# A scan layer's last unit: its sum taken part by part of the positions, its last product on two engines

## The chip, the cores and the metric

The kernel runs on one core of a Trainium2 chip. The metric is the device time of one execution in microseconds. In the text PE is TensorE, PEld its weight loads, DVE is VectorE, ACT ScalarE, POOL GpSimd, and SP the engine that issues the transfers between HBM and the on-chip memory SBUF. PSUM is the memory that TensorE writes its results to.

## The reference

Eight images of 192 channels, 64 x 64 pixels, fp32, go through four blocks one after the other: a block with a selective scan, a block without one, a second selective scan with a norm, and a block of windowed convolutions. The scan is what the change touches. For each of four directions through the image, each channel and each of 16 states:

```python
def step(h, inp):
    u_t, d_t, B_t, C_t = inp
    h = jnp.exp(d_t[..., None] * A) * h + (d_t * u_t)[..., None] * B_t[:, :, None, :]
    y = jnp.einsum('bkdn,bkn->bkd', h, C_t)
    return (h, y)
```

So a decay and an input are formed for every position and state, a first-order recurrence runs along the 4096 positions, and at every position the 16 states are multiplied by the 16 values of C and summed. Two of the four directions are the other two read backwards; the results of all are added.

## The kernel before, in words

An image is worked on as a whole before the next one starts: scan layer, the stages of the first and second block, scan layer, and then the stages behind the second scan of this image mixed with those ahead of the first scan of the next. That makes 16 scan layers in an execution. Each stage is in its own set of buffers and ends in HBM; between a scan layer and the stage behind it stand the tensors `ys` in HBM.

A scan layer (`scan_layer`) is cut into 48 units: two directions `d` (forward, then backward), eight chunks of Q = 512 positions, and three groups `v` of 128 rows (192 channels in two orders of the image). The last unit, number 47, is the backward one of the first chunk, group 2. A unit's states stand in one tile `da` of 128 partitions x 4 parts x 16 states x 128 positions; three such tiles take turns. A part (`s` or `g`) is 128 consecutive positions; in the backward direction the parts are worked on in falling order, so that the last part of unit 47 has place 0.

The loop over `k` (unit) and `j` (0 to 7) writes down by hand in which order the instructions stand; every engine runs its own in this order, and each waits only for the data and buffers that it needs. In step `j` of unit `k`:

- `scan` (L308, on DVE) runs the recurrence over 8 of the 16 states of one part, so two steps make a part. Its input is filled into PSUM by TensorE one step ahead (`fill`, L287).
- `times_c` (L319, on POOL), in every second step, multiplies a finished part by C, which `load_c` has broadcast from HBM into one of three tiles `ct`, issued by SP. Behind it, L322 (POOL too) adds the last states to the ones before them, so that 12 matmuls and a half one do for the sum instead of 16: for the first two parts the last four states, for the other two parts the last three. The product of a unit's fourth part stands in step 0 of the unit behind it.
- `add_up` (L337 and L342, on TensorE) sums the states of the unit before by matmuls with the identity into a PSUM tile `py`, of which there is one. A matmul of L337 takes one state over all four parts, 512 columns; L342 takes the thirteenth state of the last two parts, 256 columns. The list SUM says how many matmuls stand in each step.
- `load_y` (L328, SP) and `finish` (L352 or L356, DVE, and L357, SP) bring in the forward direction's result from `yp` where the unit is a backward one, add the sum to it and store the result to `ys`. `finish` of unit k stands in step 2 of unit k + 2, and `load_y` of unit k just behind `finish` of unit k - 1, in step 2 of unit k + 1. The tile `yo` has two buffers.

The loop runs over `nu + 2` = 50 places, so that the last two units are brought to their end; in the last two places there is nothing else left to do. `misc` is a PSUM tile of 512 columns with two buffers, used for transpositions (L229, L186) and small projections. The stage behind reads `ys` from HBM at L600 or L785 (or first loads weights for the next image, at L482), and it is issued by SP behind the last store at L357.

Line numbers in what follows are those of the profile of the kernel before.

Of the kernel before, what the change touches and what calls it, by code (L numbers as in the profile page):

```python
# [9 lines left out]
ALU = mybir.AluOpType  # L10
# [11 lines left out]
NS = 16  # L22
SB = 128
NB = Q // SB
# [16 lines left out]
def tile_net(ctx: ExitStack, tc: tile.TileContext, a: dict, out: bass.AP):  # L41
    nc = tc.nc
# [5 lines left out]
    ident = cst.tile([P, P], F32, name="ident")  # L48
# [50 lines left out]
    def scan_layer():  # L99
# [5 lines left out]
        with (  # L105
# [13 lines left out]
            NP = 12  # L119
            units = [  # L120
                (d, i, i if d == 0 else nck - 1 - i, v)
                for d in range(2) for i in range(nck) for v in range(3)
            ]
            vt, xd, cdr, dg = {}, {}, {}, {}
            dts, dtx, dtt, das, cts, us, py, yo = {}, {}, {}, {}, {}, {}, {}, {}

# [4 lines left out]
            def misc():  # L131
                return sp.tile([P, Q], F32, tag="misc", name="misc", bufs=2)


            def load_v(m):
                d, c, cols = chunk_of(m)
                vt[m] = sv.tile([P, 3, Q], F32, tag="vt", name="vt", bufs=3)
                for v in (2, 0, 1):
                    nc.sync.dma_start(out=vt[m][:, v, :], in_=vs[v][:, cols])
# [52 lines left out]
            def diagonals_b(m, o, r):  # L192

                shape = [P, 4, NS // 2, 32]
                at = slice(r * 4, (r + 1) * 4)
                nc.vector.tensor_tensor(  # L196
                    dg[m, o][:, at], msk[:, 0:32].unsqueeze(1).unsqueeze(1).to_broadcast(shape),
                    bts[m, o][:, at, r * 8 : r * 8 + 8].unsqueeze(3).to_broadcast(shape), ALU.mult,
                )
# [19 lines left out]
            def steps_c(k):  # L219
                dtx[k] = sw.tile([P, Q], F32, tag="dtx", name="dtx")  # L220
                nc.gpsimd.tensor_tensor(dtx[k], dts[k], vt[k // 3][:, units[k][3], :], ALU.mult)  # L221
# [27 lines left out]
            def cut(k, s=slice(0, NB)):  # L249

                d = units[k][0]
                head = das[k][:, s, :, SB - 1 if d else 0]
                nc.scalar.copy(da0[:, k % 2, s], head)
                nc.scalar.mul(head, head, 0.0)  # L254
# [39 lines left out]
            def scan(k, j):  # L294
                d, i, c, v = units[k]
                s, n = place(k, j)
                last = 0 if d else SB - 1
                u = us.pop((k, j))
                if j > 1 or i:
                    if j % 2 == 0:  # L300
                        prev = das[k][:, s + 1 if d else s - 1, :, last] if j else carry[v]
                        tmps[k] = sw.tile([P, NS], F32, tag="tmp", name="tmp")
                        nc.vector.tensor_tensor(tmps[k], da0[:, k % 2, s], prev, ALU.mult)  # L303
                    head = u[:, :, SB - 1 if d else 0]
                    nc.vector.tensor_tensor(head, head, tmps[k][:, n], ALU.add)  # L305
                way = slice(None, None, -1 if d else 1)
                h = das[k][:, s, n].rearrange("p n t -> p (n t)")[:, way]
                nc.vector.tensor_tensor_scan(  # L308
                    h, h, u.rearrange("p n t -> p (n t)")[:, way], 0.0, ALU.mult, ALU.add
                )  # L310

            def keep(k):
                d, i, c, v = units[k]
                if i < nck - 1:
                    nc.scalar.copy(carry[v], das[k][:, 0 if d else NB - 1, :, 0 if d else SB - 1])

            def times_c(k, g):
                h = das[k][:, NB - 1 - g if units[k][0] else g]
                nc.gpsimd.tensor_tensor(h, h, cts.pop((k, g)), ALU.mult)  # L319
                n = NS - NP if g < 2 else NS - NP - 1  # L320
                to = h[:, NP - n : NP]
                nc.gpsimd.tensor_tensor(to, to, h[:, NS - n : NS], ALU.add)  # L322

            def load_y(k):
                d, i, c, v = units[k]
                yo[k] = sw.tile([P, Q], F32, tag="yo", name="yo")
                if d:
                    nc.sync.dma_start(out=yo[k], in_=yp[v][:, c * Q : (c + 1) * Q])  # L328
# [3 lines left out]
            def add_up(count):  # L332

                for k, n in to_add[:count]:
                    if n == 0:
                        py[k] = sp.tile([P, Q], F32, tag="py", name="py")
                    nc.tensor.matmul(  # L337
                        py[k], ident, das[k][:, :, n, :], start=(n == 0), stop=(n == NP - 1)
                    )
                    if n == 8:  # L340
                        s = slice(0, NB // 2) if units[k][0] else slice(NB // 2, NB)
                        nc.tensor.matmul(  # L342
                            py[k][:, s.start * SB : s.stop * SB], ident, das[k][:, s, NP, :],
                            start=False, stop=False,
                        )
                del to_add[:count]

            def finish(k):
                d, i, c, v = units[k]
                p, y = py.pop(k), yo.pop(k)  # L350
                if d == 0:
                    nc.vector.scalar_tensor_tensor(  # L352
                        y, vt[k // 3][:, v, :], skip[:, v : v + 1], p, ALU.mult, ALU.add
                    )
                else:
                    nc.vector.tensor_tensor(y, y, p, ALU.add)  # L356
                nc.sync.dma_start(out=(ys if d else yp)[v][:, c * Q : (c + 1) * Q], in_=y)  # L357

            nu, nm = len(units), len(units) // 3


            SUM = ((1, 0, 1, 2, 0, 2, 1, 2), (2, 2, 1, 1, 1, 2, 2, 2), (2, 1, 1, 2, 2, 2, 2, 2))
# [2 lines left out]
            def has(k):  # L365
                return 0 <= k < nu
# [24 lines left out]
                    fill(0, 0)  # L391
            for r in range(2):
                diagonals_b(0, 1, r)
            for k in range(nu + 2):
                m, v = divmod(k, 3)
                ahead = 0 <= m + 1 < nm
                for j in range(8):
                    if v == 1 and j == 3 and 0 <= m + 2 < nm:
                        load_v(m + 2)
                    if has(k):  # L400
                        scan(k, j)
                    if j == 7:
                        if has(k + 1):
                            cut(k + 1)
                        if has(k):
                            keep(k)
                    if j % 2 == 0:
                        kk, g = (k, j // 2 - 1) if j else (k - 1, 3)
                        if has(kk):
                            times_c(kk, g)  # L410
                        if has((4 * kk + g + 3) // 4):
                            load_c(*divmod(4 * kk + g + 3, 4))
                    if j == 5 and has(k + 2):
                        steps_c(k + 2)
                    kk, jj = (k, j + 1) if j < 7 else (k + 1, 0)
                    if has(kk):
                        fill(kk, jj)
                    if j == 2:
                        if has(k - 2):
                            finish(k - 2)  # L420
                        if has(k - 1):
                            load_y(k - 1)
                        if has(k + 1):
                            turn(k + 1)
                    if ahead and (v, j) == (0, 4):

                        steps_a(k + 3)
                        steps_a(k + 4)
                    if ahead and v == 1 and j == 1:

                        steps_b(k + 2)
                        steps_a(k + 4)
                        steps_b(k + 3)
                        steps_b(k + 4)
                    if v == 0 and ahead:
                        if j == 0:
                            project_a(m + 1)
                        if j == 1:
                            project_b(m + 1)
                    if v > 0 and ahead:  # L440
                        if j == (5, 1)[v - 1]:
                            diagonals_a(m + 1, v - 1)
                        if j >= 6:
                            diagonals_b(m + 1, v - 1, j - 6)
                    if j == 2 and has(k - 1):
                        to_add += [(k - 1, n) for n in range(NP)]
                    add_up(SUM[v][j])
                    if has(k + 1) and j in DECAY:
                        decay(k + 1, *DECAY[j])

# [852 lines left out]
```

## Time and profile before

| | us |
|---|---|
| median of three runs | 26363.84 |
| the three runs | 26368.85, 26363.84, 26362.46 |
| the profiled execution | 26345.77 |
| its span, first to last instruction | 26344.0 |

| engine | busy us | share of the span |
|---|---|---|
| PE | 23298.1 | 88% |
| PEld | 12085.3 | 46% |
| DVE | 20617.9 | 78% |
| ACT | 14204.8 | 54% |
| POOL | 19170.7 | 73% |

The mean granted clock of TensorE is 0.929 of full speed. How to read it: the shares are means over stages with different limits, the scan layers and what stands between them, so a change in one place is read from the rows of that place. A matmul in fp32 stands in the records as two, and a weight load goes with each; a record's duration is longer than the distance to the next, since records overlap. In a view in order of time several records of one line are drawn together, and the brackets hold the idle time ahead of the first one and what ended it. Groups are by line; `da`, `ct`, `py`, `yo` are the tiles named above.

### The profile page before, as it was taken

Reading aid. Unit: us, or ns where it says so; the run is one execution under the profiler, and the core shown is the slowest. Engines: PE = TensorE matmul, PEld = TensorE weight load, DVE = VectorE, ACT = ScalarE, POOL = GpSimd, SP = SyncE. Lnnn points to the kernel's source line nnn. Section 1 sums busy time; section 2 is a strip of 40 time slices with the busy share of each in tenths; the row PEclk is TensorE's granted clock in tenths of the full one; section 3 lists DMA queues with packets and bytes.
Section 4 is the critical chain, followed back from the end, with each engine's and each line's share of the span. In section 5 each row is a group of like instructions: output and inputs, shape, how many; then the busy total and the mean of one; then the engine's idle time right before and its main releaser. Section 6 shows DMA issues by size and latency. Waiting matters only on the chain.

```text
span 26344.0 us, 431326 instructions
## 1 busy us (share of the span) xinstructions
PE 23298.1 (88%) x173960; PEld 12085.3 (46%) x173960; DVE 20617.9 (78%) x21237; ACT 14204.8 (54%) x23120; POOL 19170.7 (73%) x7452
## 2 busy tenths in 40 slices
PE   9979889798897988979889898898989989899896
PEld 4535445353453534535345353453535535355353
DVE  7959789597885968859688696886968869688695
ACT  5646456464554645546455464554645546465463
POOL 7929589295892958939589395893958939588395
PEclk9989999899998999989999899998999989999898
DMA  5636556265563655636556365563656636566364
GB/s 168 206 92 201 148 174 205 92 203 149 171 201 96 203 145 175 200 96 202 143 177 205 93 203 139 181 201 93 203 137 182 200 96 204 134 186 197 99 204 119
DMA packets 1204798, 4293.86 MB, mean 163 GB/s; under 512 B 360224, under 2 KB 419456, under 8 KB 804480
## 3 DMA queue, kind: packets, MB, share of 16 engines
q1 hardware_dynamic: 1202816, 4266.25, 54.7%
q8 instruction: 1388, 22.74, 0.4%
q14 instruction: 594, 4.87, 0.1%
HBM read 3810.55 MB, written 450.72 MB: 162 GB/s over the span
## 4 chain that ended last, share of the span: by engine, by line
POOL 36%; PE 12%; DVE 7%; ACT 3%; issue 3%; DMA 2%; SPq 0%; POOLq 0%; DVEq 0%; ACTq 0%
POOL da L319 27%; POOL da L322 6%; PE py L337 3%; PE pa L501 2%; POOL dtx L221 2%; PE u L287 2%; DVE da L308 2%; PE pa L504 1%; ACT da L244 1%; DVE pwc L932 1%; DVE t L966 1%; DMA a<-t 1%; DMA t<-u 0%; PE paa L501 0%; PE pb L511 0%
## 5 line engine op out<-in xcount | busy, mean ns | idle before, releaser
L308 DVE TENSOR_TENSOR_SCAN da<-da,u 128x1024 f32<-128x1024 f32 x6144 | 14039.6, 2286 | 328.7 <-ACT da L254 37.9
L319 POOL TENSOR_TENSOR da<-da,ct 128x2048 f32<-128x2048 f32 x3072 | 13928.8, 4534 | 330.6 <-DVE tmp L303 302.2
L337 PE MATMUL py<-da,ident 128*128 128x512 f32 x18432 | 9494.1, 628 | 538.8 <-POOL da L319 437.4
L287 PEld LDWEIGHTS u<-dg,dtt 32*128 32x128 f32 x131072 | 5946.8, 163 | 4601.3 <-issue 4301.7
L244 ACT ACTIVATE da<-dt,neg_a 128x512 f32<-128x512 f32 (+1 forms) x12544 | 7662.2, 699 | 16.2
L287 PE MATMUL u<-dg,dtt 32*128 32x128 f32 x131072 | 7237.6, 283 | 118.0 <-DVE da L308 49.3
L337 PEld LDWEIGHTS py<-da,ident 128*128 128x128 f32 x18432 | 3122.1, 191 | 3138.8 <-issue 2239.7
L221 POOL TENSOR_TENSOR dtx<-dt,vt 128x512 f32<-128x512 f32 x768 | 979.5, 1276 | 4011.7 <-ACT dt L217 3747.0
L322 POOL TENSOR_TENSOR da<-da 128x512 f32<-128x512 f32 (+1 forms) x3072 | 3487.6, 1135 | 240.9
L231 ACT COPY dtt<-misc 128x512 f32<-128x512 f32 x768 | 450.4, 586 | 3338.3 <-PE misc L229 3338.3
L305 DVE TENSOR_TENSOR u<-u,tmp 128x8 f32<-128x8 f32 x5952 | 1007.6, 169 | 1092.7 <-PE u L287 869.8
L234 ACT COPY dtt<-misc 32x512 f32<-32x512 f32 x3008 | 1734.7, 577 | 45.2
L196 DVE TENSOR_TENSOR dg<-msk,misc 128x1024 f32<-128x1024 f32 x1024 | 1222.6, 1197 | 442.6 <-PE misc L186 258.7
L160 ACT ACTIVATE xd<-misc,msk 128x512 f32<-128x512 f32 x256 | 175.7, 686 | 1791.3 <-PE misc L156 1791.3
L217 ACT ACTIVATE dt<-misc 128x512 f32<-128x512 f32 x768 | 430.8, 595 | 1105.1 <-PE misc L213 1098.0
L914 PE MATMUL pwc<-t,l3taps 128*128 128x486 f32 (+1 forms) x1280 | 595.3, 614 | 234.4 <-DVE t L935 214.0
L920 POOL TENSOR_TENSOR acc<-u,gate 128x486 f32<-128x486 f32 (+1 forms) x80 | 108.4, 1360 | 949.5 <-DVE u L935 674.0
L876 POOL MEMSET t<- 128x4356 f32 (+2 forms) x32 | 100.6, 3145 | 934.3 <-DVE t L850 913.4
L501 PE MATMUL pa<-sqa,mean_w 128*128 128x512 f32 x384 | 306.5, 944 | 337.1 <-ACT sqa L541 337.1
L229 PE MATMUL misc<-ident,dtx 128*128 128x128 f32 x3072 | 594.2, 318 | 0.0
L186 PE MATMUL misc<-ident,xd 16*128 16x16 f32 x4096 | 565.6, 266 | 25.2 <-DVE dg L196 25.2
L186 PEld LDWEIGHTS misc<-ident,xd 16*128 16x128 f32 x4096 | 528.2, 210 | 92.6 <-issue 88.8
(286 smaller groups left out, 18307.8 us busy)
## 6 DMA issues: line engine op xcount, KB each, us to landing
ct<-cd SPq DMA_DIRECT2D x2048, 1024.0 KB
ct<-cd SPq DMA_DIRECT2D x2048, 512.0 KB
vt<-vs SPq DMA_DIRECT2D x768, 256.0 KB
yp<-yo SPq DMA_DIRECT2D x384, 256.0 KB
yo<-yp SPq DMA_DIRECT2D x384, 256.0 KB
ys<-yo SPq DMA_DIRECT2D x384, 256.0 KB
yt<-ys SPq DMA_DIRECT2D x96, 512.0 KB
t<-ys SPq DMA_DIRECT2D x96, 512.0 KB
```

What stands on the lines that cost most here:

```text
L186: nc.tensor.transpose(pt[:, i * NS : (i + 1) * NS], xd[m][rows, cols], ident[rows, rows])
L196: nc.vector.tensor_tensor(dg[m, o][:, at], msk[:, 0:32].unsqueeze(1).unsqueeze(1).to_broadcast(shape), bts[m, o][:, at, r * 8 : r * 8 + 8] ...
L221: nc.gpsimd.tensor_tensor(dtx[k], dts[k], vt[k // 3][:, units[k][3], :], ALU.mult)
L234: (nc.scalar.copy if k else nc.vector.tensor_copy)(dtt[k][q * 32 : (q + 1) * 32, 1], pt[r * 32 : (r + 1) * 32])
L244: nc.scalar.activation(das[k][:, s, n, :], dts[k].rearrange("p (s t) -> p s t", t=SB)[:, s], AF.Exp, scale=neg_a[:, v, d, n : n + 1],)
L287: nc.tensor.matmul(u[ch, r * 4 : r * 4 + 4, e::4], dtt[k][rows, r, e, ch], dg[k // 3, o][rows, r * 4 + e, n], start=True, stop=True,)
L305: nc.vector.tensor_tensor(head, head, tmps[k][:, n], ALU.add)
L308: nc.vector.tensor_tensor_scan(h, h, u.rearrange("p n t -> p (n t)")[:, way], 0.0, ALU.mult, ALU.add)
L319: nc.gpsimd.tensor_tensor(h, h, cts.pop((k, g)), ALU.mult)
L322: nc.gpsimd.tensor_tensor(to, to, h[:, NS - n : NS], ALU.add)
L337: nc.tensor.matmul(py[k], ident, das[k][:, :, n, :], start=(n == 0), stop=(n == NP - 1))
L501: nc.tensor.matmul(pa[:, h], w[0][:, c], src[0][:, h], start=True, stop=False)
```

## The change

For the last unit of each layer alone:

- Its sum is not made by `add_up` but by a new function `add_last`, part by part: the first two parts together (12 matmuls of 256 columns), then the third (13 of 128 columns), then the fourth (16 of 128 columns). It goes into a `misc` tile instead of the `py` tile.
- The product of its fourth part by C is cut in two: 8 states on POOL and 8 on DVE. The addition of L322 isn't made for this part.
- `load_y` of this unit stands in step 3 of the unit itself, and `finish` in step 2 of place 48. The loop has 49 places instead of 50.

The first two parts are summed behind the last full step of the unit, that is before the last matmul of unit 46; the third and fourth behind it.

```diff
--- before.py
+++ after.py
@@ -121,6 +121,7 @@
                 (d, i, i if d == 0 else nck - 1 - i, v)
                 for d in range(2) for i in range(nck) for v in range(3)
             ]
+            nu, nm = len(units), len(units) // 3
             vt, xd, cdr, dg = {}, {}, {}, {}
             dts, dtx, dtt, das, cts, us, py, yo = {}, {}, {}, {}, {}, {}, {}, {}
 
@@ -316,6 +317,12 @@
 
             def times_c(k, g):
                 h = das[k][:, NB - 1 - g if units[k][0] else g]
+                if k == nu - 1 and g == NB - 1:
+
+                    ct = cts.pop((k, g))
+                    for eng, n in ((nc.gpsimd, slice(0, 8)), (nc.vector, slice(8, NS))):
+                        eng.tensor_tensor(h[:, n], h[:, n], ct[:, n], ALU.mult)
+                    return
                 nc.gpsimd.tensor_tensor(h, h, cts.pop((k, g)), ALU.mult)
                 n = NS - NP if g < 2 else NS - NP - 1
                 to = h[:, NP - n : NP]
@@ -345,6 +352,19 @@
                         )
                 del to_add[:count]
 
+            def add_last(g0, g1):
+
+                k = nu - 1
+                if k not in py:
+                    py[k] = misc()
+                s = slice(NB - g1, NB - g0)
+                ns = NS if g1 == NB else NP + (g0 == 2)
+                for n in range(ns):
+                    nc.tensor.matmul(
+                        py[k][:, s.start * SB : s.stop * SB], ident, das[k][:, s, n, :],
+                        start=(n == 0), stop=(n == ns - 1),
+                    )
+
             def finish(k):
                 d, i, c, v = units[k]
                 p, y = py.pop(k), yo.pop(k)
@@ -356,7 +376,6 @@
                     nc.vector.tensor_tensor(y, y, p, ALU.add)
                 nc.sync.dma_start(out=(ys if d else yp)[v][:, c * Q : (c + 1) * Q], in_=y)
 
-            nu, nm = len(units), len(units) // 3
 
 
             SUM = ((1, 0, 1, 2, 0, 2, 1, 2), (2, 2, 1, 1, 1, 2, 2, 2), (2, 1, 1, 2, 2, 2, 2, 2))
@@ -391,7 +410,7 @@
                     fill(0, 0)
             for r in range(2):
                 diagonals_b(0, 1, r)
-            for k in range(nu + 2):
+            for k in range(nu + 1):
                 m, v = divmod(k, 3)
                 ahead = 0 <= m + 1 < nm
                 for j in range(8):
@@ -418,7 +437,9 @@
                     if j == 2:
                         if has(k - 2):
                             finish(k - 2)
-                        if has(k - 1):
+                        if k == nu:
+                            finish(k - 1)
+                        if has(k - 1) and k < nu:
                             load_y(k - 1)
                         if has(k + 1):
                             turn(k + 1)
@@ -442,9 +463,17 @@
                             diagonals_a(m + 1, v - 1)
                         if j >= 6:
                             diagonals_b(m + 1, v - 1, j - 6)
-                    if j == 2 and has(k - 1):
+                    if (k, j) == (nu - 1, 3):
+                        load_y(k)
+                    if j == 2 and has(k - 1) and k < nu:
                         to_add += [(k - 1, n) for n in range(NP)]
                     add_up(SUM[v][j])
+                    if (k, j) == (nu - 1, 7):
+                        add_last(0, 2)
+                    if (k, j) == (nu, 0):
+                        add_up(NP)
+                        add_last(2, 3)
+                        add_last(3, 4)
                     if has(k + 1) and j in DECAY:
                         decay(k + 1, *DECAY[j])
```

## The prediction

> **What bounds the kernel now.** I read the page first, then the busy time of the engines by stage, then the end of a scan layer in order of time, because the edits of this change touch only the last of a layer's 48 units. From the page, the costliest groups (out<-in, count, busy us, mean ns, idle before it and its releaser):
>
> ```profile
> L308 DVE TENSOR_TENSOR_SCAN da<-da,u 128x1024 f32<-128x1024 f32 x6144 | 14039.6, 2286 | 328.7 <-ACT da L254 37.9
> L319 POOL TENSOR_TENSOR da<-da,ct 128x2048 f32<-128x2048 f32 x3072 | 13928.8, 4534 | 330.6 <-DVE tmp L303 302.2
> L337 PE MATMUL py<-da,ident 128*128 128x512 f32 x18432 | 9494.1, 628 | 538.8 <-POOL da L319 437.4
> L322 POOL TENSOR_TENSOR da<-da 128x512 f32<-128x512 f32 (+1 forms) x3072 | 3487.6, 1135 | 240.9
> ```
>
> Within a layer a unit costs POOL four products and four additions, 4 x (4.534 + 1.135) = 22.7 us, and almost no product waits: 330.6 us of idle over 3072. So POOL paces the units, and nothing here changes one of them but the last. What matters is that TensorE waited 437.4 us for L319 in all, part of it in each layer's end. That end, at the first layer, from the view in order of time (start, duration, engine, line; idle before it in brackets):
>
> ```profile
> 1337.73 2.29 DVE L308 TENSOR_TENSOR_SCAN da<-da,u 128x1024 f32<-128x1024 f32 x1
> 1339.20 0.59 PE L342 MATMUL py<-da,ident 128*128 128x256 f32 x2
> 1339.63 2.74 PE L337 MATMUL py<-da,ident 128*128 128x512 f32 x6
> 1340.09 4.51 POOL L319 TENSOR_TENSOR da<-da,ct 128x2048 f32<-128x2048 f32 x1
> 1342.41 0.69 DVE L356 TENSOR_TENSOR yo<-yo,py 128x512 f32<-128x512 f32 x1 [2.39 <-PE py L337]
> ...
> 1344.65 7.99 PE L337 MATMUL py<-da,ident 128*128 128x512 f32 x18 [2.28 <-POOL da L319]
> ...
> 1355.69 0.69 DVE L356 TENSOR_TENSOR yo<-yo,py 128x512 f32<-128x512 f32 x1 [12.59 <-PE py L337]
> 1356.40 0.32 SPq L357 DMA_DIRECT2D ys<-yo  x1
> 1358.70 1.27 SPq L600 DMA_DIRECT2D yt<-ys  x3
> ```
>
> Count from the end of the last scan, 1340.02 = 0. TensorE is still summing unit 46 until +2.4, stands until the last product of unit 47 ends at +4.6 (every matmul of `add_up` reads all four parts of the positions), then sums unit 47 without a break: 26 records, +4.64 to +15.64. DVE adds the first direction (+15.7), the store leaves, and the next stage's first load is issued 2.3 us behind the store. Nothing else runs in this stretch, so every us that the last matmul moves, the rest of the kernel moves. The 16 layers' ends, measured alike: the last addition at L356 starts at +15.67 to +15.74 in 11, +16.59 in the last, +17.37 in two, +18.77 and +20.42 in two. The last four lost time to the TensorE clock; by stage (columns: us, busy time and count of PE, PEld, DVE, ACT, POOL, then PEclk, DMA share, GB/s):
>
> ```profile
> 1342.20:1344.70 2.50, 0.22 (x2) 0.05 (x1) 0.69 (x1) 0.00 (x0) 2.42 (x2) 1.00 0.33 111
> 17727.40:17731.60 4.20, 0.21 (x2) 0.06 (x1) 0.69 (x1) 0.00 (x0) 4.12 (x2) 0.91 0.46 116
> 17731.60:17735.00 3.40, 3.40 (x4) 1.46 (x5) 0.00 (x0) 0.00 (x0) 0.96 (x1) 0.50 0.03 11
> 17737.70:17745.60 7.90, 7.88 (x20) 3.41 (x18) 0.00 (x0) 0.00 (x0) 0.00 (x0) 1.00 0.00 0
> ```
>
> The first row is the wait at a usual end, the second the wait of 4.2 us at the layer that ended at +20.42; behind it the granted clock is 0.50 for about 6 us.
>
> **The change, part by part.** *Sums by part.* Removed: 12.5 full-width matmuls of unit 47 behind the product. A matmul has two records; two of 512 columns start 0.429 us apart (2.74 for six: (2.74 - 0.59)/5 = 0.43), two of 256 columns 0.216 (from the record starts at L342: 1339.201, 1339.417, next 1339.633). Added: 12 matmuls of 256 columns for the first two parts, 13 of 128 for the third, 16 of 128 for the fourth, so 24, 26 and 32 records. Their order on TensorE is: unit 46's matmuls 9 and 10, the 24, unit 46's matmul 11, the 26, the 32. The record of matmul 11 starts at 1341.35 = +1.33 now; there the 24 begin. Their inputs are long ready: the product of the second part and its additions ended before 1334.41 = -5.6, where the third part's product starts. The third part's product ends at 1338.93 and its addition at 1340.01.
>
> The 24 records take 24 x 0.215 = 5.16, to +6.49. Matmul 11 takes 2 x 0.429 = 0.86, to +7.35. For 128 columns with 128x128 weights the trace of before has no matmul of this kind. From below: streaming scales with the columns (0.429, 0.215), so 0.107. The nearest row is the transposition at L229, 128x128 by 128 columns, whose four records, each with a weight load of its own, start 0.120 to 0.122 apart once running. The same 0.12 appears at L186 with only 16 columns:
>
> ```profile
> 24756.10 0.75 PE L186 MATMUL misc<-ident,xd 16*128 16x16 f32 x5 [1.53 <-DVE dg L196]
> ```
>
> Five records of 0.27 in 0.75 us are (0.75 - 0.27)/4 = 0.12 each: the pace of the weight load, whatever is streamed. I take 0.120: 58 x 0.120 = 6.96, to +14.31, and the last record ends 0.16 later, +14.47. Against +15.64 that is 1.17 us less at a usual end: 2.45 of standing and 0.1 of restart are removed, 1.4 is added because 82 narrow records cost 12.1 us where 26 wide ones cost 10.7.
>
> Here the Trainium skill speaks against the change. "TensorE: Matmul & The Clock Gate", section "LDWEIGHTS (loading the stationary operand)", prices a load at its columns over 1.2 per ns, 107 ns for 128 columns. If load and matmul ran one behind the other, a record would cost 0.107 + 0.107 = 0.213, the 58 would take 12.4, and the end would be at +19.9: 4.2 us later than now. The rows at L229 and L186 have both together in 0.12, so the load runs beside the previous matmul and I use 0.12. The end breaks even at 0.12 + 1.17/58 = 0.140.
>
> *The split product.* Now 4.51 us on POOL from +0.07. Afterwards POOL does 8 of 16 states, 4.53/2 = 2.27, from the end of its previous addition, about 0 to +2.3; DVE does the other 8 (1.22 us by L628, 128x1024 with both inputs in SBUF) behind its last scan, to about +1.3. The addition behind it (1.00) goes. TensorE reaches this part at +7.35 + 26 x 0.12 = +10.5. So the split saves nothing on the path, and costs nothing: even if the two halves ran one behind the other, +3.5. Its cover is 8 us. On DVE only the additions of units 46 and 47 are queued behind, and they are late anyway.
>
> *Unit 46's addition* moves from +2.39 to about +7.5 because matmul 11 stands behind the 24 records. Its store is issued at about +8.3 and lands some 2 us later (2.3 from store to next load above), well before unit 47's. Zero.
>
> *The earlier load of yp.* It is moved on SP from behind the addition of unit 46 to behind unit 46's own load, one step after it. It needs the buffer of unit 45, whose store left just before; SP then waits about 2 us, and the only instruction queued behind is the store of unit 46, some 10 us later. No load of C is left. Zero; the addition of unit 47 waited for TensorE, not for this load.
>
> *The tile of its own.* The sum goes into one of the two "misc" tiles, last used by transpositions of unit 47 and long read out by ScalarE. Zero. Neither a step of the unit loop nor a transfer is added.
>
> *The sum, at full clock.* 16 x 1.17 = 18.7. In three ends the product came late, so TensorE's standing was 1.71, 1.70 and 0.91 us longer; the new order depends on the part before, and gains that too: 4.3. Together 23.0.
>
> *The clock.* The four slow ends lost 20.42 - 15.7 - 1.71 = 3.0, 18.77 - 15.7 - 1.70 = 1.4, and 1.7 twice: 7.8. The skill's same page, "HAM oscillation — how this bites in real kernels", says that a gap over about 3.4 us makes the clock fall to half. The trace agrees for the two gaps of 4.2 us (0.50 afterwards); of the 13 gaps of about 2.4, two fell too, so here a shorter gap can do it. As the change leaves no gap, the rule gives back the 7.8 and the sum is 30.8; if the clock falls at random, it is 23. I take 30.8.
>
> The profiled execution took 26345.77 (span 26344.0 and 1.8 around it); less 30.8 is 26315. The median of the runs is 18.1 higher, and I subtract from it: 26363.8 - 30.8 = 26333, 0.12% less. A measurement of this kernel tells about 0.2% (53 us) from no change.
>
> **The rivals.**
> 1. *Narrow matmuls at streaming pace* (0.107): 58 x 0.013 = 0.75 more per layer, 12; gain 43, 26321. For it: L287's narrow records; against: L229.
> 2. *TensorE waits after all*, for POOL's half product before the first 24 (a wait that covers more than its own part): the 24 begin at +2.3 instead of +1.33, 16 us of the gain go, 26348. The region written by the half is not read by the 24, which speaks against it.
> 3. *Loads not hidden*, the other side: 0.213 a record costs 58 x 0.093 = 5.4 more per layer, 86; 30.8 - 86 = 55 slower, 26419. It decides from 0.12 + 30.8/928 = 0.153 on; 0.2% slower is reached at 0.21. Against it are L229 and L342 (0.216 with loads of 0.19 hidden).
> 4. *The change does nothing visible*: the next stage waits for something other than unit 47's store. Then 26364. Against it: the first load is issued 2.3 us behind that store, with nothing between.
>
> **How the numbers follow.** The likeliest case with the clock's uncertainty (23 to 31) has 0.60; rival 1 0.17; rival 2 0.11; rival 3 0.06; rival 4 0.06. The range runs from rival 1 less 17 for runs that differ (the profiled execution is 18 below the median) to rival 4 and a little, leaving out rival 3: 26304 to 26368. Over 0.2% faster needs 3.3 us per layer, which no case reaches alone; rival 1 with such a difference does: 0.08. Slower by over 0.2% is about rival 3: 0.05. Within: 0.87.
>
> **What would show it.** In the profile after: no TensorE gap between the last fill and the last sum of a layer; records of the 128-column sums 0.12 apart; the last addition at about +14.5 in all 16 ends, none behind a half clock; unit 46's addition near +7.5; the DVE product ending before +2. Wrong, if those records are 0.15 or more apart, if the gap is back before the first 256-column record, or if the first load of the next stage no longer follows the store.

## The result, and the profile after

| | before, us | after, us |
|---|---|---|
| median of 15 runs | 26363.78 | 26320.19 |
| lowest to highest | 26332.23 to 26392.23 | 26293.51 to 26357.69 |
| span of the profiled execution | 26344.0 | 26318.4 |

The ratio is 0.9983 with a 95% interval of 0.9975 to 0.9991: 24 to 66 us less, 43.6 by the medians. Against 26333 forecast, 26320 was measured; it lies within the forecast range, and within 0.2% of no change.

Single executions spread over some 60 us, more than the whole effect. What the change does is read from the 16 ends of the scan layers instead. The first of them in order of time, from the profile of the changed kernel (start, duration, engine, line; idle before it in brackets; L363 is `add_last`, L324 the split product, L376 the addition of the first direction):

```profile
1335.39 2.29 DVE L309 TENSOR_TENSOR_SCAN da<-da,u 128x1024 f32<-128x1024 f32 x1
1336.04 2.36 POOL L324 TENSOR_TENSOR da<-da,ct 128x1024 f32<-128x1024 f32 x1
1337.30 1.88 PE L344 MATMUL py<-da,ident 128*128 128x512 f32 x4
1337.71 1.77 DVE L324 TENSOR_TENSOR da<-da,ct 128x1024 f32<-128x1024 f32 x1
1339.01 5.34 PE L363 MATMUL misc<-da,ident 128*128 128x256 f32 x24
1344.19 1.02 PE L344 MATMUL py<-da,ident 128*128 128x512 f32 x2
1345.05 6.64 PE L363 MATMUL misc<-da,ident 128*128 128x128 f32 x58
1345.25 0.69 DVE L376 TENSOR_TENSOR yo<-yo,py 128x512 f32<-128x512 f32 x1 [5.78 <-PE py L344]
...
1351.73 0.69 DVE L376 TENSOR_TENSOR yo<-yo,misc 128x512 f32<-128x512 f32 x1 [5.79 <-PE misc L363]
1354.74 3.23 SPq L629 DMA_DIRECT2D yt<-ys  x6
```

The last scan ends at 1337.68, which is 0 below. TensorE has no gap any more: four records of unit 46 from -0.38 on, the 24 from +1.33 on, the two of matmul 11, and the 58, one behind the other. Unit 46's addition is at +7.57, the last one at +14.05 where it was at +15.7. The next stage's first load still stands 3.0 us behind the start of the last addition, as before. The three rows by stage are the stretch with the 24 records of 256 columns in this end, its 128-column records, and the end at which TensorE had stood longest before the change, 3.99 us (columns: us, busy time and count of PE, PEld, DVE, ACT, POOL, then PEclk, DMA share, GB/s):

```profile
1338.00:1344.00 6.00, 6.00 (x27) 4.77 (x26) 1.48 (x1) 0.00 (x0) 0.40 (x1) 1.00 0.00 0
1345.05:1351.69 6.64, 6.64 (x59) 6.44 (x57) 0.69 (x1) 0.00 (x0) 0.00 (x0) 1.00 0.10 39
17718.40:17732.40 14.00, 13.94 (x88) 11.93 (x86) 2.52 (x3) 0.00 (x0) 0.73 (x1) 1.00 0.05 19
```

TensorE is busy throughout and the granted clock is 1.00, in the third row too, where the end took 20.4 us before and had 0.50 for 6.8 of them. In the second row the weight loads are busy 6.44 of 6.64 us: more below. In the groups of the whole execution, TensorE's idle time ahead of the old sum that POOL's products ended fell from 437.4 to 399.6 us:

```profile
L344 PE MATMUL py<-da,ident 128*128 128x512 f32 x18048 | 9316.2, 628 | 497.3 <-POOL da L326 399.6
```

All 16 last additions start at +14.05. Added up, these starts are 263.1 us in the profile before and 224.8 in the one after, 38.3 less, which lies within the interval of 24 to 66. The two spans differ by only 25.6, so the rest of the execution was 12.7 longer in this pair (26093.6 against 26080.9). In the eight further profiles below that rest lies anywhere from 26037 to 26088, so single executions differ by more than this, and a pair of spans is no measure of this change.

### The profile page after: what moved, and what is told of

The parts are those of the page before. It is cut to its first block, busy times and chain, and to the rows that moved or that the text cites. A ratio compares the mean times of both kernels' runs of the same rounds, so it can differ in the third digit from the quotient of the medians.

```text
span 26318.4 us, 433127 instructions
## 1 busy us (share of the span) xinstructions
PE 23311.1 (89%) x174856; PEld 12180.1 (46%) x174856; DVE 20653.6 (78%) x21253; ACT 14200.1 (54%) x23120; POOL 19119.8 (73%) x7436
## 4 chain that ended last, share of the span: by engine, by line
POOL 35%; PE 13%; DVE 7%; ACT 4%; issue 3%; DMA 2%; SPq 0%; POOLq 0%; DVEq 0%; ACTq 0%
POOL da L326 26%; POOL da L329 6%; PE py L344 3%; PE pa L530 2%; PE u L288 2%; POOL dtx L222 2%; DVE da L309 2%; ACT da L245 1%; PE pa L533 1%; DVE pwc L961 1%; DVE t L995 1%; DMA a<-t 1%; PE misc L363 0%; DMA t<-u 0%; PE pac L530 0%
## 5 line engine op out<-in xcount | busy, mean ns | idle before, releaser
L344 PE MATMUL py<-da,ident 128*128 128x512 f32 x18048 | 9316.2, 628 | 497.3 <-POOL da L326 399.6
L344 PEld LDWEIGHTS py<-da,ident 128*128 128x128 f32 x18048 | 3045.9, 191 | 2995.1 <-issue 2134.2
L329 POOL TENSOR_TENSOR da<-da 128x512 f32<-128x512 f32 (+1 forms) x3056 | 3471.0, 1136 | 239.7
```

The lines of the kernel that those rows point to most:

```text
L344: nc.tensor.matmul(py[k], ident, das[k][:, :, n, :], start=(n == 0), stop=(n == NP - 1))
```

## The experiments

For each run the table gives the start of the last addition behind the last scan, over the 16 ends, their sum, and how many ends had a stretch of half clock (a granted clock of 0.50) in TensorE's sum. Where there is a ratio, it is to the kernel before on the same chip; the other runs have one execution each, whose time tells nothing here.

| kernel | last addition at | sum of 16 | half clock | ratio (95%) |
|---|---|---|---|---|
| before | 15.67 to 20.42 | 263.1 | 4 | |
| after | 14.05 | 224.8 | 0 | 0.9983 (0.9975 to 0.9991) |
| whole product | 13.38 | 214.1 | 0 | |
| halves | 13.19 | 211.0 | 0 | 0.9984 (0.9976 to 0.9991) |
| split alone | 14.23 to 17.78 | 243.8 | 3 | |
| split, own tile | 13.13 to 17.78 | 238.7 | 4 | |
| load back | 14.05 | 224.8 | 0 | |
| gap | 14.55 to 20.44 | 268.5 | 8 | |
| narrower | 17.57 | 281.1 | 0 | |
| fold | 9.30 to 11.21 | 158.5 | 0 | 0.9965 (0.9951 to 0.9978) |

**The last product left whole.** Against the changed kernel:

```diff
-                if k == nu - 1 and g == NB - 1:
...
-                        eng.tensor_tensor(h[:, n], h[:, n], ct[:, n], ALU.mult)
-                    return
...
-                ns = NS if g1 == NB else NP + (g0 == 2)
+                ns = NP + (g0 >= 2)
```

> The changed kernel with the last product left whole on POOL, with its addition, so that the fourth part is summed by 13 matmuls instead of 16. All times from the end of a layer's last scan; the last addition starts at +14.05 in the changed kernel. Theory (TensorE's own work sets the end, the split is hidden): 6 narrow records of 0.112 us fewer, so +13.4 in all 16 ends, though the product now ends at +4.5 to +7.2. Rival (the split product is what ends the layer earlier): later than +14.05, by up to the 2.3 us that the other half takes.

Measured: 13.38 in all 16 ends, with the product ending between +4.59 and +6.30. That is the theory's number, to 0.02. So the split is not only without use on the path: it cost three matmuls, 0.67 us per layer, since the fourth part does without POOL's addition and is summed over 16 states.

**The split alone**, in the kernel before:

```diff
-                nc.gpsimd.tensor_tensor(h, h, cts.pop((k, g)), ALU.mult)
+                if k == nu - 1 and g == NB - 1:
+                    ct = cts.pop((k, g))
+                    for eng, n in ((nc.gpsimd, slice(0, 8)), (nc.vector, slice(8, NS))):
+                        eng.tensor_tensor(h[:, n], h[:, n], ct[:, n], ALU.mult)
+                else:
+                    nc.gpsimd.tensor_tensor(h, h, cts.pop((k, g)), ALU.mult)
```

> The kernel before with one part of the change, the last product split over POOL and DVE; its addition stays, and so does the sum over all four parts at once into the one py tile. Theory: the first matmul of unit 47 can now start when unit 46's addition has freed the tile, at +3.1, or when the later half of the product is done where that is later (up to +5); so the last addition at 3.1 + 0.1 + 10.7 + 0.2 = +14.1 where the product is early, up to +16 where it is late. Rival (only the sum by parts helps): +15.7 as before.

Measured: +14.23 to +14.24 in four ends with an early product, +14.55 to +14.56 in five, +15.13 to +15.38 in four, and +17.76 to +17.78 in three whose sum ran partly at half clock. The second layer's end, whose last scan ends at 2965.34, from the view in order of time (L323 is the split product, L343 the sum, L362 the addition):

```profile
2963.80 2.35 POOL L323 TENSOR_TENSOR da<-da,ct 128x1024 f32<-128x1024 f32 x1
...
2965.37 1.85 DVE L323 TENSOR_TENSOR da<-da,ct 128x1024 f32<-128x1024 f32 x1
...
2967.73 0.69 DVE L362 TENSOR_TENSOR yo<-yo,py 128x512 f32<-128x512 f32 x1 [0.51 <-PE py L343]
...
2968.57 7.96 PE L343 MATMUL py<-da,ident 128*128 128x512 f32 x18 [0.87 <-DVE yo L362]
```

Both halves are done by 2967.22, but the sum waits for unit 46's addition to read the tile out. The split does shorten a layer where the sum stands behind the product, and its gain depends on when POOL gets to it.

**The split with a tile of its own**, one line more:

```diff
-                        py[k] = sp.tile([P, Q], F32, tag="py", name="py")
+                        py[k] = misc() if k == nu - 1 else sp.tile([P, Q], F32, tag="py", name="py")
```

> As the run with the split alone, but unit 47's sum goes into a misc tile, as in the changed kernel; still all four parts at once. Theory: the wait for unit 46's addition goes, the sum starts when the split product is done, +0.7 to +5, but not before unit 46's own sum ends at +2.2: the last addition at +13.2 in the best ends and up to +16 in the late ones, the spread of POOL's half showing through. Rival (the tile of its own is worth nothing): the same as with the split alone.

Measured: +13.13 in three ends, where the sum follows unit 46's without a gap; +13.38 to +13.40 in three; +14.55 in five, +15.36 in one, and +17.75 to +17.78 in four with half clock. The tile is worth 1.1 us where the product is early (14.23 to 13.13). At its best this order ends 0.9 earlier than the changed kernel, since 26 wide records take 10.7 us and the 82 narrow ones 11.7; on average it ends later (14.9 against 14.05), because it still waits for POOL's half in ten ends, and in four of them half clock follows. The end at the ninth layer by stage, wait, half clock and rest:

```profile
14432.80:14436.00 3.20, 0.51 (x2) 0.30 (x2) 0.69 (x1) 0.00 (x0) 3.20 (x3) 1.00 0.47 127
14436.10:14439.50 3.40, 3.40 (x6) 1.33 (x5) 0.00 (x0) 0.00 (x0) 0.38 (x1) 0.51 0.11 34
14439.50:14448.30 8.80, 8.77 (x22) 3.83 (x20) 0.00 (x0) 0.00 (x0) 0.00 (x0) 1.00 0.00 0
```

**The third and fourth part together**, against the run with the whole product:

```diff
-                        add_last(2, 3)
-                        add_last(3, 4)
+                        add_last(2, 4)
```

> As the run with the whole product, but the third and fourth part are summed together, 13 matmuls of 256 columns instead of 13 and 13 of 128. Theory (TensorE's records set the end): 24 x 0.216, 2 x 0.429 and 26 x 0.216 from +1.33, so the last record ends near +13.2 and the last addition starts there, in all 16 ends; 0.85 us less than the changed kernel per layer, 14 us in all, 0.05%, below what the timing can tell. Rival (narrow records are as cheap as wide ones for the same columns): +13.4, as with the whole product.

Measured: 13.19 in all ends. The rival falls by 0.19 us, which is 26 x (2 x 0.1117 - 0.216) = 0.19: the same columns cost a little less in wide records. The ratio of 0.9984 can't be told from the changed kernel's, as expected.

**Narrower still**, to see what holds a narrow record. Against the changed kernel, the fourth part in two halves of 64 columns:

```diff
+                if g1 == NB:
+                    for t0 in (0, SB // 2):
+                        for n in range(ns):
+                            nc.tensor.matmul(
+                                py[k][:, t0 : t0 + SB // 2], ident, das[k][:, 0, n, t0 : t0 + SB // 2],
...
```

> The changed kernel with the fourth part summed in two halves of 64 columns, 64 records instead of 32, the same columns in all. The 128-column records stand 0.1117 us apart in the changed kernel, between the streaming price (0.107) and the 0.12 of the transpositions, so that run does not say what holds them. Theory A (the weight load of 128 columns paces a narrow record, whatever is streamed): 64 columns are no cheaper than 128, 0.11 to 0.12 a record, so the end is 32 x 0.11 = 3.5 later, last addition at +17.6 to +18.1. Theory B (they are held by streaming alone): 0.056 a record, last addition at +14.1.

Measured: 17.57 in all ends, theory A. In order of time, and the 64-column stretch by stage:

```profile
1348.26 3.06 PE L371 MATMUL misc<-da,ident 128*128 128x128 f32 x26
...
1351.16 7.26 PE L365 MATMUL misc<-da,ident 128*128 128x64 f32 x64
```

```profile
1351.21:1358.42 7.21, 7.20 (x65) 7.06 (x64) 0.00 (x0) 0.00 (x0) 0.00 (x0) 1.00 0.01 2
```

64 records of 64 columns take twice what 32 of 128 took; nearly all start 0.111 or 0.112 us apart, as the 128-column ones do, while weight loads are busy 7.06 of 7.21 us. So a record of this kind costs 0.112 us at least, however few columns it streams, and its load runs beside the matmul before it. That the load is what holds it is inferred from how busy the loads are; a sum with fewer weight columns was not run. A fixed price of every record it is not: in the same profiles records of `fill`, whose weights fill 32 rows, start as little as 0.007 us apart.

**The load at its old place.** Against the changed kernel:

```diff
+                        if has(k - 1):
+                            load_y(k - 1)
                         if k == nu:
                             finish(k - 1)
-                        if has(k - 1) and k < nu:
-                            load_y(k - 1)
...
-                    if (k, j) == (nu - 1, 3):
-                        load_y(k)
```

> The changed kernel with the load of yp for unit 47 at its old place, behind unit 46's addition and ahead of unit 47's. Theory: unit 46's addition starts at +7.6, its store is issued at +8.3, the load at +8.7 and it lands some 2 to 3 us later, before the sum ends; the last addition at +14.05 as in the changed kernel. Rival (the earlier load is needed because unit 46's addition is late now): the last addition waits for the transfer and starts later than +14.1.

Measured: 14.05 in all ends. Moving the load earlier is worth nothing in this order.

**A gap put in.** Against the changed kernel:

```diff
                     ct = cts.pop((k, g))
+                    for w in (NS, NS, 8):
+                        spare = sw.tile([P, NS, SB], F32, tag="ct", name="ct", bufs=3)
+                        nc.gpsimd.tensor_tensor(spare[:, :w], ct[:, :w], ct[:, :w], ALU.mult)
```

> The changed kernel with three products more on POOL ahead of its half of the last one (two of 2048 and one of 1024 elements per partition, into a free ct tile, used by nothing): about 11.3 us. TensorE is through with the third part at +10.3 and must wait for POOL's half, which now ends between +12 and +16.3, so gaps of 1.8 to 6 us stand in front of the last 32 records. Theory on the clock (a gap makes it fall): with an idle time of about 2.8 us or more the half clock follows in most ends, and the 32 records take up to 7.2 us instead of 3.6; with less it follows seldom. Rival (it falls at random, or from work): half clock in at most 4 of the 16 ends, as in the kernel before, whatever the gap. The last addition at +16 to +20 at full clock, up to 3.5 later at half.

Measured: POOL's half ended at +10.6 to +14.0, earlier than expected (a product of a tile with itself took 3.60 us instead of 4.53, the one of half the size 1.89), so TensorE stood for at most 3.58 us. Half clock followed in 8 ends, all behind a gap of 1.86 us or more, of which there were 11; in none of the 5 with 0.38 us or less. The rival had at most 4, whatever the gap; it falls. But the boundary expected, 2.8 us, was too high. The largest gap and the sum behind it, by stage:

```profile
21018.70:21022.30 3.60, 0.11 (x1) 0.00 (x0) 0.00 (x0) 0.00 (x0) 3.60 (x2) 0.81 0.00 0
21022.30:21028.80 6.50, 6.38 (x32) 6.19 (x32) 0.00 (x0) 0.00 (x0) 0.04 (x1) 0.58 0.01 3
```

Over all ten profiles of this case (a gap is the longest idle time of TensorE between the last fill and the last sum):

| gap | ends with half clock behind it |
|---|---|
| none (0.1 us at most) | 0 of 91 |
| 0.11 to 1.78 us | 0 of 33 |
| 1.86 to 2.35 us | 8 of 24 |
| 2.66 us and more | 11 of 12 |

The length of the gap alone does not decide, and the traces show what else counts. In all ten, every stretch of equal granted clock, but for the last one that the end of the trace cuts off, lasts a whole multiple of 3.413 us, so each trace has a fixed grid of windows of that length at whose bounds the clock changes. Three ends of the kernel before, cut at these bounds (same columns as above): the sixth layer's with a gap of 2.28 us, the tenth's with the same gap, and the last with 3.20 us:

```profile
9518.39:9521.80 3.41, 2.42 (x6) 0.76 (x4) 0.75 (x2) 0.00 (x0) 3.27 (x1) 1.00 0.00 0
9521.80:9525.21 3.41, 2.12 (x5) 1.06 (x6) 0.00 (x0) 0.00 (x0) 2.23 (x2) 1.00 0.54 154
```

```profile
16078.80:16082.22 3.42, 1.14 (x4) 0.31 (x3) 0.69 (x1) 0.00 (x0) 3.34 (x2) 1.00 0.26 90
16082.22:16085.63 3.41, 3.41 (x5) 1.35 (x5) 0.00 (x0) 0.00 (x0) 0.78 (x1) 0.50 0.28 64
```

```profile
25922.84:25926.25 3.41, 1.75 (x5) 0.45 (x3) 0.69 (x1) 0.00 (x0) 3.41 (x2) 1.00 0.02 7
25926.25:25929.67 3.42, 1.88 (x5) 0.93 (x6) 0.00 (x0) 0.00 (x0) 2.48 (x2) 1.00 0.53 146
```

In the first and the third a bound parts the gap: TensorE is busy for more than half of each window and the clock stays, even with 3.20 us. In the second the gap falls into one window: TensorE is busy for a third of it, and the next window has half clock. The shares part all 160 ends: of the windows that end before the last record of the sum, the least busy one was 0.00 to 0.456 busy in the 19 ends with half clock, and 0.459 or more in the other 141. It is a pattern found in the records afterwards, not a forecast that was tested, and not the whole rule: over the whole executions half clock followed all 1965 full-clock windows that were under 0.40 busy, but also some between 0.40 and 0.85.

**Work taken away from TensorE.** The end is TensorE's own work now, and DVE stands idle beside it. Against the changed kernel:

```diff
+            def fold(s0, s1, n1):
+                t = das[nu - 1]
+                lo, hi = t[:, s0:s1, 0 : n1 - 8], t[:, s0:s1, 8:n1]
+                nc.vector.tensor_tensor(lo, lo, hi, ALU.add)
...
+                    fold(2, 4, 12)
                     for eng, n in ((nc.gpsimd, slice(0, 8)), (nc.vector, slice(8, NS))):
                         eng.tensor_tensor(h[:, n], h[:, n], ct[:, n], ALU.mult)
+                    fold(1, 2, NS)
+                    fold(0, 1, NS)
...
+                if k == nu - 1 and g == 2:
+                    return
...
+                ns = 8
...
-                        add_last(2, 3)
-                        add_last(3, 4)
+                        add_last(0, 2)
+                        add_last(2, 4)
```

> A version that takes work from TensorE in the end, since DVE has nothing to do there: DVE adds states 8 to 11 of the first two parts onto 0 to 3 (in the changed kernel POOL has left 12), and states 8 to 15 of the third and of the fourth part onto 0 to 7; POOL's addition for the third part goes. TensorE then sums 8 states by matmuls of 256 columns, twice, behind unit 46's last matmul: 32 records instead of 82. Theory (TensorE's records set the end): 2.2 + 32 x 0.216 = +9.1 and 0.2, so +9.3 where the folded states are ready in time; DVE's four operations of 1.2 us and POOL's half get in each other's way, which can put the fourth part off to +6 or +7.5 and the last addition to +10 or +11. Against 263 us of ends in the kernel before 150 to 175: 90 to 115 us less, 0.34 to 0.44%. Rival (the end is set by something else from there on, the products or the store): not below +12.

Measured: +9.30 in three ends, +9.64 to +9.85 in ten, +10.61 in one and +11.21 in two. From the first layer's end, whose last scan ends at 1335.24 (L321 is the folding, L329 the split product, L372 the sum):

```profile
1334.29 2.34 POOL L329 TENSOR_TENSOR da<-da,ct 128x1024 f32<-128x1024 f32 x1
...
1335.16 2.56 DVE L321 TENSOR_TENSOR da<-da 128x1024 f32<-128x1024 f32 x1
1337.64 1.21 DVE L329 TENSOR_TENSOR da<-da,ct 128x1024 f32<-128x1024 f32 x1
1337.87 7.14 PE L372 MATMUL misc<-da,ident 128*128 128x256 f32 x32 [0.27 <-DVE da L321]
1338.78 2.35 DVE L321 TENSOR_TENSOR da<-da 128x1024 f32<-128x1024 f32 x2
```

The 32 records run as one; the first folding took 2.56 us, as POOL was in its product for the first 1.5 of them. The ends sum to 158.5, 104.7 less than before, and the medians differ by 101.3 (26232.34 against 26333.62; interval 58 to 129). As far as this interval tells, what the ends give reaches the time whole. By the point estimates this version is the fastest of all; its interval is clear of no change and only touches the changed kernel's.

## Why the prediction was right, step by step

*TensorE's own work sets the end; standing is exchanged for narrower records.* Right, and shown: the end moves with the records alone. Six fewer narrow ones (whole product) give 0.67 us, 32 more (narrower) 3.52, 26 wide for 52 narrow (halves) 0.19.

*The size of one term was off.* A 128-column record was taken at 0.120 from the transpositions; it is 0.1117. 58 x 0.0083 = 0.48, and the last record ended at +14.01 instead of +14.47. Over 16 layers that is 7.4 us: the ends gave 38.3 instead of 30.8. The time came out 13 us under the forecast, 7.4 of it from here; the rest is within the spread of the runs.

*The weight load paces a narrow record, beside the matmul.* Right that streaming isn't what holds it: 64 columns cost what 128 do. The prediction's price for a load and a matmul one behind the other (0.213) is refuted; the Trainium skill's figure for a load alone ("TensorE: Matmul & The Clock Gate", section "LDWEIGHTS (loading the stationary operand)"), 107 ns for 128 columns, is near the 0.112. Rival 1 named the measured median, 26321, by luck: it gave the ends 42.8 us where they gave 38.3, and the rest is the spread of the runs. Its reason is wrong too: the record is near the streaming price only because 128 columns stream in about the time below which such a record does not fall.

*The clock.* All of the 7.8 us came back, in this execution as in every one without a gap; no gap and no half clock went together in 91 of 91 ends. The step "a gap over about 3.4 us makes it fall" is too narrow. The gaps that the prediction calls 2.4 and 4.2 us hold 0.1 to 0.2 us of matmul each (idle: 2.28 to 2.35 and 3.99); gaps of 1.86 to 2.35 us did it in 8 of 24 ends and one of 3.20 us did not. The other case that the prediction allowed, a clock that falls at random, does not fit the records either: how the gap lies to the clock's windows tells the ends with half clock from the others.

*The split product costs nothing and saves nothing on the path.* Right that it saves nothing, wrong that it costs nothing: without POOL's addition, the fourth part needs 16 matmuls instead of 13, 0.67 us per layer, which the forecast did count as records but not as the split's price. The bound of +3.5 for both halves was also too low: they ended at up to +5.0, because POOL came to its half at up to +2.66. And DVE's half, forecast to end before +2, ended at 2.06 in one end and at 3.38 to 3.40 in four. From one of these, the changed kernel's ninth layer:

```profile
14436.47 2.35 POOL L324 TENSOR_TENSOR da<-da,ct 128x1024 f32<-128x1024 f32 x1
14436.53 3.37 DVE L324 TENSOR_TENSOR da<-da,ct 128x1024 f32<-128x1024 f32 x1
```

DVE's half takes 1.22 us where it starts first and 3.37 where POOL is 0.06 ahead, ending just 1.08 behind it; the other way round POOL's takes 3.34 instead of 2.36. The one that is second stands still, as the Trainium skill has it ("SBUF — State Buffer", section "SBUF: two separate sides": VectorE with two SBUF inputs and GpSimd exclude each other for a whole instruction). TensorE comes to this part at +10.3 only, so none of it reaches the end.

*Unit 46's addition, the moved load.* As forecast: +7.57 for +7.5, and nothing. *The tile of its own* was costed at zero as a price, which holds, but its worth was not asked for: in the order of the run with the split alone it saves 1.1 us. What it saves in the changed kernel's own order was not tried.

## What to carry to other kernels

At the end of a stage, ask which engine's work is left once the waits are gone: here removing the wait for a product was worth only what TensorE's longer, narrower sum left of it, and taking work off TensorE gave nearly three times as much. Cutting a sum into narrower parts has a price that grows as the parts shrink: for the same columns 0.19 us at 128 columns against 256, but 3.52 us at 64 against 128, more than the usual gap of 2.28 us that the change removed. Where an effect is below the spread of the runs, read the stretch that the change touches in every repetition within one execution: 16 ends that agree to 0.01 us say more than the span. And where an engine's clock falls behind a gap, look at how the gap lies to the bounds at which the clock changes before taking its length for the cause.

## What the runs showed that was not expected

Gaps of TensorE of only 1.86 to 2.05 us brought half clock in 6 of 9 ends of one run, and one of 3.20 us in the kernel before brought none. And an early DVE operation can do harm: put ahead of POOL's product it makes the product 1 us longer, put just behind it, it takes 3.4 us itself.
